# A Mamba-style mixer on one core: VectorE's work inside a phase put in another order

## Chip, cores and metric

One NeuronCore of a Trainium2 chip runs the whole program in one launch. The metric is the device time of one execution in microseconds (us), as a median of runs. PE is the matrix engine TensorE, DVE is VectorE, ACT is ScalarE, POOL is GpSimd and SP is the engine that issues most DMAs.

## What is computed

Four residual blocks follow one another on x (1024 tokens by 512, as 2 sequences b of 512), all in float32. The third takes most of the time:

```python
x = x + block_sparse(layernorm(x))     # weight masked in 32x32 blocks, plus bias
x = x + ffn(layernorm(x))              # dequantised int weights, 512 -> 1792 -> 512
x = x + mixer(layernorm(x))            # 128 heads of 64 channels, state of 128, 8 groups
x = x + ffn(layernorm(x))
# mixer, of one head, with chunks of 128 tokens:
xc, B, C = silu(conv4(x_proj)), silu(conv4(B_proj)), silu(conv4(C_proj))
y = (mask * exp(decay) * (C B^T)) @ (dt*xc)  +  C @ states * exp(decay)  +  D*xc
out += (rmsnorm(y) * norm_w * silu(gate)) @ out_w
```

## The kernel before

**Tiles and phases.** The 8192 channels of the mixer are 64 tiles of 128. A *phase* `ph` handles two of them for both sequences, so four *units* (j, b): tile j, sequence b. `units` (line 782) lists them as (0,0), (0,1), (1,0), (1,1). Phases are pipelined three deep. In one pass of the loop at line 1156 PE does four things: the input projection of the new pair of tiles (`x_front`), the scan of the pair before it, the output projection of the pair before that (`out_seven`, 14 small products called `o()`), and the gate projection of the new pair (`g_front`).

**Seven products.** A projection for two tiles and two sequences is a Strassen-Winograd scheme, `seven` (line 177): a generator of seven products (x, y, z, then y, x, y, z again, adding to the same three PSUM banks). Between them ACT copies the first one (L202) and DVE adds (L206 after the second product; L211 and L212 after the fourth; L220 after the sixth; L225 after the seventh). The fourth and sixth products write into a bank that DVE has just read, so the fourth waits for L206 and the sixth for L211.

**A unit's work.** `conv` (ACT, L731) and three taps on DVE (L734, queued in a list and issued by `drain(n)`), then `silu` (ACT). `x_tokens` (called `tokens(k)`, k an index into `units`) turns the x tile into tokens with four PE transposes (L827) into a PSUM bank with the tag "tr", of which there are two; DVE multiplies it by dt (L831), POOL by the decay (L835). `states` makes the chunk states on PE (L848) and carries them from chunk to chunk on DVE (one copy L859 and four small operations L862). `scores` makes the decays of one head on ACT (L892, L899, L902); their product with the masked C B^T, L900, is put into the list `mults` and issued by `flush()`, which empties the list; POOL multiplies `ce` (L906). `scan` is 28 small matmuls of a unit (L919, L928); `skipped` adds D*xc (L939) and `gated` multiplies by the gate (L942), both on DVE. `squares` adds y squared (ACT L948, POOL L949); its y buffer is one of three.

**Kinds of phase.** Every fourth phase also projects B and C of the next group (`group`, another seven products on PE with 12 taps); here it is called a *group phase* (`new_group`, ph = 3, 7, ... 27). The phase after it makes that group's masked C B^T in `group_scores` (a *post-group phase*). The other 15 phases from 2 to 30 are called *plain*. The branch `if mid:` (line 1216) holds the order of all of these.

**What sets the order.** `manual_schedule` (line 1540) keeps PE, ACT and DVE in the order in which the program issues, so a waiting instruction holds up all that follows on its engine. POOL and SP are ordered by the framework.

**Ends.** In `block_sparse` the weight's four row blocks are masked by `masked(kc)` (line 322): a row sum on DVE, a small matmul `pb`, a comparison and a multiplication L333, for the last block on POOL. After the last phase the code from line 1459 finishes the mixer: the last pair's output projections (`last_outs(t)`, 8 of them), the residual and norm of token tiles 0 to 3 (`rest`, `ahead`) and their transposes (`turn`).

Of the kernel before, what the change touches and what calls it, by code (L numbers as in the profile page):

```python
# [11 lines left out]
ALU = mybir.AluOpType  # L12
AX = mybir.AxisListType

P = 128
# [18 lines left out]
PP = 2  # L34
# [3 lines left out]
def kernel(  # L38
# [251 lines left out]
    def block_sparse():  # L290

        with tc.tile_pool(name="bs", bufs=1) as pool:
# [29 lines left out]
            def masked(kc):  # L322
# [9 lines left out]
                eng = nc.gpsimd if kc == KC - 1 else nc.vector  # L332
                eng.tensor_tensor(wv, wv, on.unsqueeze(2).to_broadcast([P, NB, 32]), ALU.mult)  # L333
# [18 lines left out]
            normed = [h() for h in halves]  # L352
            next(mask[0])
            for n in normed:
                turn(n)
            next(mask[0])
            pos = [bs_o() for _ in range(2)]
            for kc in range(KC):
                product(0, pos[0], kc)
                if kc + 1 < KC:  # L360
                    next(mask[kc + 1])
                product(1, pos[1], kc)
                if kc + 1 < KC:
                    next(mask[kc + 1])
# [304 lines left out]
    def mixer(waiting, step_args, loaded):  # L669

        with ExitStack() as st:
# [110 lines left out]
            units = [(j, b) for j in range(PP) for b in range(2)]  # L782
# [60 lines left out]
            def states(ct, b, x_dec, b_tok, by_act):  # L843
# [12 lines left out]
                if by_act:  # L856
                    nc.scalar.copy(state[:, 0], pst[:, 0])
                else:
                    nc.vector.tensor_copy(state[:, 0], pst[:, 0])  # L859
                for c in range(1, NCH - 1):  # L860
                    for hh in range(2):
                        nc.vector.scalar_tensor_tensor(  # L862
                            state[:, c, hh, :],
                            state[:, c - 1, hh, :],
                            e_last[:, b, c - 1, h0 + hh : h0 + hh + 1],
                            pst[:, c, hh, :],
                            ALU.mult,
                            ALU.add,
                        )
                return state  # L870
# [7 lines left out]
            def flush():  # L878
                for f in mults:
                    f()  # L880
                mults.clear()
# [274 lines left out]
            for ph in range(1, n_ph + 1):  # L1156
# [23 lines left out]

                def tokens(k):
# [3 lines left out]
                def both_states(k, by_act=False):  # L1185
                    for j, b in units[2 * k : 2 * k + 2]:
                        sts[j, b] = states(c1 + j, b, xts[j, b][1], groups[c1 // CTG][b][1], by_act)
# [26 lines left out]
                tokens(0)  # L1214
                tokens(1)
                if mid:
# [8 lines left out]
                    tokens(2)  # L1225
                    tokens(3)
                    flush()
                    o()
                    next(steps)
                    back_scores(2)  # L1230
                    o()
# [397 lines left out]
```

## Time and profile before

| | |
|---|---|
| median of 3 runs | 2297.31 us (2296.64 to 2298.96) |
| the profiled execution's own time | 2297.72 us |
| its span, first to last instruction | 2296.0 us |
| PE / DVE / POOL / ACT busy | 98% / 81% / 56% / 51% |
| span of a post-group phase, two plain ones and a group phase, one after the other | 52.10, 48.70, 49.20, 61.60 us |
| DVE busy in those four | 46.12, 45.08, 45.75, 54.86 us |

Times inside the profile are counted from the start of its span. A fenced line of a timeline gives start, duration, engine, line of the kernel, operation and tiles, the number of instructions put together, and in brackets how long the engine sat idle before them and on whom it waited. A line of the waits gives who waited for whom: the sum in us, how often, the longest. A row of the windows gives a stretch and its length, then each engine's busy time with its number of instructions, TensorE's granted clock, the DMA engines' busy share and GB/s. Matmuls overlap in the records, so the spacing of their starts tells more than their duration.

### The profile page before, as it was taken

The numbers are of one execution on the slowest core, as the hardware profiler recorded it, in microseconds if no ns is written. First come the engines' busy times: TensorE is split into PE (matmuls) and PEld (weight loads), VectorE is DVE, ScalarE is ACT, GpSimd is POOL, SyncE is SP. The second block draws the span as 40 slices with busy tenths as digits, with TensorE's granted clock in tenths as the row PEclk, the third lists the DMA queues.
The fourth block names the chain that finished last, engine by engine and source line by source line (L and its number), as shares of the span: only waits on it lengthen the run. The fifth ranks groups of instructions, "written<-read, shape, count | busy, mean of one in ns | idle before, by whom it ended". The sixth has DMA issues, their size and how long they took to land.

```text
span 2296.0 us, 30153 instructions
## 1 busy us (share of the span) xinstructions
PE 2248.0 (98%) x10704; PEld 1403.4 (61%) x10704; DVE 1850.8 (81%) x3103; ACT 1168.9 (51%) x2474; POOL 1277.3 (56%) x1203
## 2 busy tenths in 40 slices
PE   9999999999999999999999999999999999999999
PEld 5444865656665665666666656665666666544468
DVE  5456568888998999899889989998998899865553
ACT  4111056756565665666566656655665666631100
POOL 3665024756655666566657565665675665527620
PEclk9999999999999999999999999999999999999999
DMA  5663022222222222222222222221222322427600
GB/s 178 196 199 113 24 70 64 74 73 66 74 74 65 74 78 79 65 74 83 65 74 69 70 73 70 77 85 56 83 74 65 101 74 74 120 83 226 203 21 28
DMA packets 145783, 201.59 MB, mean 88 GB/s; under 512 B 7136, under 2 KB 92000, under 8 KB 145632
## 3 DMA queue, kind: packets, MB, share of 16 engines
q1 hardware_dynamic: 145056, 198.61, 27.0%
q8 instruction: 85, 1.39, 0.2%
q10 hardware_dynamic: 576, 1.05, 0.1%
q14 instruction: 66, 0.54, 0.1%
HBM read 194.91 MB, written 4.72 MB: 87 GB/s over the span
## 4 chain that ended last, share of the span: by engine, by line
PE 77%; DVE 20%; ACT 2%; issue 1%; DMA 1%; POOL 0%; ACTq 0%; SPq 0%; POOLq 0%; DVEq 0%
PE proj L185 25%; PE po L1020 13%; PE yo L185 13%; PE ffn_o L556 7%; DVE m L900 5%; PE py L919 4%; PE pst L848 3%; DVE xc L734 3%; PE py L928 3%; DVE x_sb L1034 2%; DVE gt L942 2%; PE x_tr L827 2%; PE po L956 2%; PE pg L486 1%; PE pu L486 1%
## 5 line engine op out<-in xcount | busy, mean ns | idle before, releaser
L906 POOL TENSOR_TENSOR ce<-ce,c_t 128x384 f32<-128x384 f32 x256 | 299.5, 1174 | 343.0 <-ACT ce L902 337.2
L185 PE MATMUL proj<-xn_t,w 128*128 128x512 f32 x824 | 384.6, 593 | 2.0 <-DVE gt L206 1.7
L892 ACT ACTIVATE m<-bc,acs 128x128 f32<-128x128 f32 x1024 | 324.8, 389 | 8.3 <-PE py L919 8.2
L900 DVE TENSOR_TENSOR m<-m,gm 128x512 f32<-128x512 f32 x256 | 254.0, 1010 | 16.4 <-ACT m L899 16.4
L185 PEld LDWEIGHTS proj<-xn_t,w 128*128 128x128 f32 x824 | 153.0, 190 | 146.4 <-issue 136.0
L1034 DVE TENSOR_TENSOR x_sb<-x_sb,po 128x512 f32<-128x512 f32 x340 | 229.7, 682 | 15.6 <-PE po L1020 9.6
L734 DVE SCALAR_TENSOR_TENSOR xc<-proj,cw,xc 128x511 f32<-128x511 f32 (+2 forms) x288 | 214.8, 746 | 6.6
L171 POOL TENSOR_TENSOR ws<-w 128x256 f32<-128x256 f32 x96 | 72.9, 759 | 238.3 <-DMA w<-in_win_t_dram 195.5
L185 PE MATMUL proj<-tq,ws 128*128 128x512 f32 x432 | 199.3, 592 | 0.0
L919 PE MATMUL py<-m,x_dt 128*64 128x128 f32 x2048 | 189.1, 277 | 3.3 <-DVE m L900 3.2
L949 POOL TENSOR_TENSOR sq_acc<-sq_acc,y 128x512 f32<-128x512 f32 x128 | 179.6, 1406 | 20.9 <-ACT y L948 20.8
L1020 PE MATMUL po<-wo,gt 128*128 128x256 f32 x696 | 177.0, 384 | 0.0
L899 ACT ACTIVATE m<-m 128x512 f32<-128x512 f32 x256 | 161.3, 630 | 7.4
L185 PE MATMUL yo<-xn_t,w 128*128 128x512 f32 x328 | 152.5, 597 | 9.0 <-DVE tmp L206 7.3
L185 PE MATMUL yo<-tq,ws 128*128 128x512 f32 x336 | 154.0, 601 | 0.2 <-ACT acs L714 0.2
L928 PE MATMUL py<-ce,state 128*64 128x128 f32 x1536 | 154.1, 273 | 0.0
L919 PEld LDWEIGHTS py<-m,x_dt 128*64 128x64 f32 x2048 | 130.8, 137 | 36.8 <-issue 25.8
L948 ACT ACTIVATE y<-y 128x512 f32<-128x512 f32 x128 | 76.5, 622 | 140.5 <-DVE gt L942 140.5
L1020 PEld LDWEIGHTS po<-wo,gt 128*128 128x128 f32 x696 | 125.4, 190 | 30.8 <-issue 9.4
L245 POOL TENSOR_TENSOR w<-w,sf 128x1024 f32<-128x1024 f32 (+1 forms) x30 | 70.0, 2335 | 111.8 <-DVE w L244 86.1
L902 ACT ACTIVATE ce<-bc 128x384 f32<-128x384 f32 x256 | 129.7, 507 | 0.0
L185 PEld LDWEIGHTS proj<-tq,ws 128*128 128x128 f32 x432 | 81.8, 190 | 76.7 <-issue 73.7
(227 smaller groups left out, 4585.1 us busy)
## 6 DMA issues: line engine op xcount, KB each, us to landing
bc<-acs_d SPq DMA_DIRECT2D x128, 512.0 KB, 3.8
w<-in_win_t_dram SPq DMA_DIRECT2D x64, 512.0 KB, 3.8
wo<-in_wo_t_dram SPq DMA_DIRECT2D x31, 512.0 KB, 5.0
wi<-in_down_w_dram SPq DMA_DIRECT2D x14, 512.0 KB, 3.8
zi<-in_down_z_dram SPq DMA_DIRECT2D x14, 512.0 KB, 4.7
sf<-in_down_s_dram SPq DMA_DIRECT2D x14, 512.0 KB, 4.3
wi<-in_gate_w_dram SPq DMA_DIRECT2D x13, 512.0 KB, 4.2
zi<-in_gate_z_dram SPq DMA_DIRECT2D x13, 512.0 KB, 5.2
```

Source lines behind the costliest of these rows:

```text
L185: nc.tensor.matmul(ps, lhsT=a[:, kc, :], rhs=b[:, kc, :], start=(start and kc == 0), stop=(stop and kc == KH - 1), skip_group_check=True,)
L556: nc.tensor.matmul(ps, lhsT=a[:, k, :], rhs=b(k), start=(start and k == 0), stop=(stop and k == KF - 1), skip_group_check=True,)
L734: nc.vector.scalar_tensor_tensor(dst[:, s:], ps[:, : SEQ - s], cw[:, t, 3 - s : 4 - s], dst[:, s:], ALU.mult, ALU.add)
L892: nc.scalar.activation(m[:, c, :], bc[:, hh, c * P : (c + 1) * P], AF.Relu, bias=acs[:, t, h : h + 1], scale=-1.0,)
L899: nc.scalar.activation(m, m, AF.Exp, scale=-1.0)
L900: mults.append(lambda: nc.vector.tensor_mul(m, m, shared[b][2]))
L906: nc.gpsimd.tensor_mul(ce, ce, c_t[:, P:].rearrange("p (c l) -> p c l", l=P))
L919: nc.tensor.matmul(py[hh * HD : (hh + 1) * HD, c * P : (c + 1) * P], lhsT=x_dt[:, c, hh, :], rhs=m[:, c, :], start=True, stop=(c == 0),)
L928: nc.tensor.matmul(py[hh * HD : (hh + 1) * HD, c * P : (c + 1) * P], lhsT=state[:, c - 1, hh, :], rhs=ce[:, c - 1, :], start=False, stop=True,
L949: nc.gpsimd.tensor_add(sq_acc[:, b, :], sq_acc[:, b, :], y)
L1020: nc.tensor.matmul(banks[k][:, c, :], lhsT=a[:, t], rhs=b, start=(start and c == 0), stop=stop, skip_group_check=True,)
L1034: nc.vector.tensor_add(q, q, banks[k])
```

## The change

In a phase between the second and the next to last: the list of units becomes (0,0), (1,1), (1,0), (0,1). The x tiles are turned after the first input product and the first output product, the second two after the second of each, and no longer around the first. The states of the second two units are made on PE where they were, or after `group_scores` in a post-group phase, but carried on DVE later, between the output products that follow the first scan. `flush(n)` can issue a part of `mults`. Both `gated` of the first scan come later, with one `squares` each. The first *two* products of the gate projection come ahead of the second scan; in a group phase the group's seven products come there with `gated` and `mults` between them. Both `gated` of the second scan come after both `skipped`. One of two `mults` of the next pair is left to the next phase. `group_scores` of the second sequence moves to the end of a post-group phase. In `block_sparse` all four multiplications are DVE's and each row sum is issued earlier; after the last phase the norms, transposes and squares stand in another order.

```diff
@@ -329,8 +329,7 @@
...
                 wv = wt[:, kc].rearrange("p (b j) -> p b j", j=32)
-                eng = nc.gpsimd if kc == KC - 1 else nc.vector
-                eng.tensor_tensor(wv, wv, on.unsqueeze(2).to_broadcast([P, NB, 32]), ALU.mult)
+                nc.vector.tensor_tensor(wv, wv, on.unsqueeze(2).to_broadcast([P, NB, 32]), ALU.mult)
                 yield
...
@@ -350,18 +349,20 @@
...
             normed = [h() for h in halves]
             next(mask[0])
+            next(mask[1])
             for n in normed:
...
             for kc in range(KC):
+                if kc + 2 < KC:
+                    next(mask[kc + 2])
                 product(0, pos[0], kc)
...
                 product(1, pos[1], kc)
-                if kc + 1 < KC:
-                    next(mask[kc + 1])
             ahead = norm(2, True)()
...
@@ -779,7 +780,8 @@
...
 
-            units = [(j, b) for j in range(PP) for b in range(2)]
+            units = [(0, 0), (1, 1), (1, 0), (0, 1)]
 
...
@@ -840,7 +842,7 @@
...
 
-            def states(ct, b, x_dec, b_tok, by_act):
+            def states(ct, b, x_dec, b_tok):
 
...
@@ -853,21 +855,21 @@
...
                 state = wrk.tile([P, NCH - 1, 2, HD], F32, name="state", bufs=4)
-                if by_act:
-                    nc.scalar.copy(state[:, 0], pst[:, 0])
-                else:
+                def carried():
                     nc.vector.tensor_copy(state[:, 0], pst[:, 0])
-                for c in range(1, NCH - 1):
-                    for hh in range(2):
-                        nc.vector.scalar_tensor_tensor(
-                            state[:, c, hh, :],
-                            state[:, c - 1, hh, :],
-                            e_last[:, b, c - 1, h0 + hh : h0 + hh + 1],
-                            pst[:, c, hh, :],
-                            ALU.mult,
-                            ALU.add,
-                        )
-                return state
+                    for c in range(1, NCH - 1):
+                        for hh in range(2):
+                            nc.vector.scalar_tensor_tensor(
+                                state[:, c, hh, :],
+                                state[:, c - 1, hh, :],
+                                e_last[:, b, c - 1, h0 + hh : h0 + hh + 1],
+                                pst[:, c, hh, :],
+                                ALU.mult,
+                                ALU.add,
+                            )
+                return state, carried
 
...
@@ -875,10 +877,12 @@
...
 
-            def flush():
-                for f in mults:
+            def flush(n=None):
+                n = len(mults) if n is None else min(n, len(mults))
+                for f in mults[:n]:
                     f()
-                mults.clear()
+                del mults[:n]
 
...
@@ -1178,13 +1182,22 @@
...
 
+                def a_square():
+                    squares(*ys.pop(0))
                 def tokens(k):
...
 
-                def both_states(k, by_act=False):
+                def both_states(k, now=True):
+                    carry = []
                     for j, b in units[2 * k : 2 * k + 2]:
-                        sts[j, b] = states(c1 + j, b, xts[j, b][1], groups[c1 // CTG][b][1], by_act)
+                        sts[j, b], carried = states(c1 + j, b, xts[j, b][1], groups[c1 // CTG][b][1])
+                        if now:
+                            carried()
+                        else:
+                            carry.append(carried)
+                    return carry
 
...
@@ -1211,8 +1224,6 @@
...
                     wbc = load_group((c0 + PP) // CTG)
-                tokens(0)
-                tokens(1)
                 if mid:
...
@@ -1222,19 +1233,21 @@
...
                     next(steps)
-                    tokens(2)
-                    tokens(3)
-                    flush()
                     o()
+                    tokens(0)
+                    tokens(1)
                     next(steps)
...
                     o()
+                    tokens(2)
+                    tokens(3)
                     o()
...
                     next(steps)
-                    flush()
+                    flush(len(mults) - 1)
                     both_states(0)
                     o()
+                    flush()
                     next(steps)
...
@@ -1245,64 +1258,96 @@
...
                     run(steps)
-                    both_states(1)
+                    if not made:
+                        carry = both_states(1, False)
                     scans = half_scan(units[:2])
...
                     o()
-                    flush()
                     back_scores(5)
                     o()
+                    flush(1)
                     o()
-                    o()
-                    gated[0]()
-                    flush()
                     back_scores(6)
...
                     o()
-                    flush()
+                    flush(1)
+                    if made:
+                        carry = both_states(1, False)
+                    carry[0]()
+                    o()
                     back_scores(7)
-                    if made:
-                        group_scores(made, groups[c0 // CTG], [1])
                     o()
-                    flush()
-                    gated[1]()
-                    all_squares()
-                    made = None
+                    carry[1]()
+                    gate, later = g_front(wg, gts_new, "proj" if new_group else ("proj", "yo", "yo"))
                     if new_group:
...
                         steps, made = group((c0 + PP) // CTG, wbc, "yo")
-                        for i, _ in enumerate(steps):
-                            if i in (1, 3, 5):
-                                drain(3)
-                        gate, later = g_front(wg, gts_new)
+                        next(steps)
+                        flush(1)
+                        gated[0]()
+                        flush(1)
+                        next(steps)
+                        drain(3)
+                        a_square()
+                        next(steps)
+                        next(steps)
+                        drain(3)
+                        gated[1]()
+                        a_square()
+                        next(steps)
+                        next(steps)
+                        run(steps)
+                        drain(3)
                     else:
-                        gate, later = g_front(wg, gts_new, ("proj", "yo", "yo"))
+                        next(gate)
+                        flush(1)
+                        gated[0]()
+                        flush(1)
+                        half_scores(0, c0, heads_new)
+                        a_square()
                         next(gate)
...
                     wo = load_out(ph - 1)
-                    finish(half_scan(units[2:], "tr"))
+                    scans = half_scan(units[2:], "tr")
+                    scans[0][0]()
+                    if new_group:
+                        scans[1][0]()
+                        next(gate)
+                        half_scores(0, c0, heads_new)
+                        next(gate)
+                    else:
+                        gated[1]()
+                        scans[1][0]()
+                    half_scores(1, c0, heads_new)
+                    if not new_group:
+                        a_square()
+                    for _, f in scans:
+                        f()
                     if ph < n_ph - 2:
                         lefts, rights = out_left(gts), out_right(wo)
-                    if new_group:
-                        next(gate)
-                    half_scores(0, c0, heads_new)
-                    next(gate)
                     drain(3)
-                    half_scores(1, c0, heads_new)
+                    for u in units[:2]:
+                        silu(xcs_new[u], xcs_new[u])
                     next(gate)
                     next(gate)
+                    flush(1)
+                    if made and not new_group:
+                        group_scores(made, groups[c0 // CTG], [1])
+                        made = None
+                    silu(xcs_new[units[2]], xcs_new[units[2]])
                     drain(3)
-                    for u in units:
-                        silu(xcs_new[u], xcs_new[u])
-                    flush()
+                    silu(xcs_new[units[3]], xcs_new[units[3]])
+                    next(gate)
                     next(gate)
...
                 else:
+                    tokens(0)
+                    tokens(1)
                     next(steps)
...
@@ -1489,35 +1534,27 @@
...
             back_scores(7)
+            flush()
             factors(0)
+            first_rest = rest(0)
             last_outs(2)
-            flush()
-            half = rest(0)
-            def ahead(t):
-                nonlocal half
-                new = rest(t + 1)
-                normed = half()
-                half = new
-                return normed
             scans = half_scan(units[2:], "proj")
-            normed = ahead(0)
+            second_rest = rest(1)
+            normed = first_rest()
             finish(scans)
...
             turn(normed)
-            normed = ahead(1)
+            normed = second_rest()
+            all_squares()
             last_outs(4)
+            halves = [rest(2), rest(3)]
+            last_outs(5)
             turn(normed)
-            normed = ahead(2)
-            last_outs(5)
-            all_squares()
-            turn(normed)
-            normed = half()
+            normed = [h() for h in halves]
             last_outs(6)
-            turn(normed)
+            turn(normed[0])
             last_outs(7)
+            turn(normed[1])
             for f in adds:
...
             factors(1)
```

## The prediction

> **What bounds the kernel now.** I read first the page's busy times, then the waits of PE, then the windows of four successive phases, then one plain phase's timeline of DVE and PE.
>
> ```profile
> PE 2248.0 (98%) x10704; PEld 1403.4 (61%) x10704; DVE 1850.8 (81%) x3103; ACT 1168.9 (51%) x2474; POOL 1277.3 (56%) x1203
> ...
> L900 DVE TENSOR_TENSOR m<-m,gm 128x512 f32<-128x512 f32 x256 | 254.0, 1010 | 16.4 <-ACT m L899 16.4
> ```
>
> PE is idle for 2296.0 - 2248.0 = 48.0 us in all. No reordering can give much more than that: the floor is near 2248.
>
> ```profile
> PE x_tr L827 <- DVE x_dt L831: 14.6, 21, 1.2
> PE yo L185 <- DVE tmp L206: 7.3, 7, 1.0
> PE ln_tr L142 <- ACT tmp L127: 4.2, 3, 2.2
> PE py L919 <- DVE m L900: 3.2, 15, 0.2
> PE bs_o L337 <- POOL wt L333: 1.9, 1, 1.9
> PE yo L185 <- DVE gt L206: 1.8, 8, 0.3
> ```
>
> Most of PE's waits are for DVE: for the second pair of x tiles (both "tr" banks full until L831), and for L206. These are what the change aims at.
>
> ```profile
> 828.30:877.50 49.20, 48.54 (x266) 31.55 (x265) 45.75 (x77) 31.26 (x69) 32.90 (x32) 1.00 0.24 75
> ```
>
> In this plain phase DVE is busy for 45.75 of 49.20 us. It has only 3.4 us to spare, so what it does while PE scans matters as much as PE's own gaps.
>
> ```profile
> 850.77 0.29 DVE L859 COPY state<-pst 128x128 f32<-128x128 f32 x1
> ...
> 853.98 0.75 DVE L939 SCALAR_TENSOR_TENSOR y<-xc,dsk,py 128x512 f32<-128x512 f32 x1 [0.28 <-PE py L928]
> ...
> 859.65 1.50 DVE L900 TENSOR_TENSOR m<-m,gm 128x512 f32<-128x512 f32 x1
> ...
> 867.34 1.68 DVE L942 SCALAR_TENSOR_TENSOR gt<-y,nw,gt 128x512 f32<-128x512 f32 x1
> ...
> 871.76 0.68 DVE L211 TENSOR_TENSOR gt<-gt,yo 128x512 f32<-128x512 f32 x1
> ```
>
> The carries (L859, L862) now fill DVE while PE does the first scan (850.55 to 853.76); from its second y (853.98) to the gate projection's L211 (872.44) DVE hardly rests. That chain of 18.46 us is the thing to follow.
>
> **The change, part by part.** The sum is made against the profiled execution's 2297.72 us, 1.7 of it outside the span; the median is 0.4 less.
>
> *Plain phases (15).* Matmuls are neither added nor removed. Today's waits of PE, from the spacing of its starts in this phase: 0.53 at the turn of x; 0.65 in the second scan (3.86 us against 3.21 for the first); 0.37 before the gate's fourth product. The phase before it has the last two only, so 1.3 on the mean. The turn's wait goes: x_dt then has an input product, an output product and eight transposes of cover (1.72 + 0.86 + 0.87 us). If that cover failed, the 0.53 would come back. The gate's wait for L206 goes too, as 3.2 us of scan now lie behind its second product.
>
> What is late next is L211. In the new order DVE does between its second y and L211 all that it does now (seven adds, four m, four gt, two y, one L206, three taps), and also both carries, which leave the shadow of the first scan. A carry takes 1.09 us (850.77 to 851.86), two 2.18. The y itself can't come earlier, since it waits for the scan: DVE idles there instead, in a gap that was the carries'. The four m and four gt last 8.46 us in this phase; with the page's mean of 1.010 and the groups' mean of 0.959 for L942 they last 7.88, so 0.58 less. Chain: 18.46 + 2.18 - 0.58 = 20.06 us. It starts 3.43 us after the first scan starts, so L211 ends at 23.5. PE would reach the gate's sixth product, which needs L211, at 873.20 - 850.55 - 0.65 - 0.37 = 21.6. It waits 23.5 + 0.1 - 21.6 = 2.0, against 1.3 now: +0.65 a phase, +9.8 in all. Part of that wait may fall earlier, where the second scan's last unit needs the fourth m (about 15.3 against 14.7); it is the same chain and counts once.
>
> [...] the change moves `gated` towards its own squares on POOL. The rows: m 0.68 alone (863.35), 1.50 beside POOL, 1.010 on the mean. [...] I take the row's mean.
>
> The other moves: the two flushes of the next pair's m become one before and one after the phase's end (0.7 to 1.0 us; at the start DVE idles 1.1 us at its L206, which hides it; uncovered it costs its full time, once a phase). The y buffers (three): the fourth y needs the first one's square; that ends, with ACT's 2.3 us of scores ahead and POOL's 1.4, near 17, and is needed near 17.8: nothing, up to 0.5 if ACT is late. `half_scores` takes its DMA of bc along (3.8 us to landing on SP, which the program doesn't order): no ACT wait for it is in the trace, so nothing. `load_pair` and `load_out` stand behind two products instead of one; POOL's sums for the output (four of 1.27 us) start some 2 us later and end about when the next phase starts, 5 us before their use: nothing, or the excess.
>
> *Post-group phases (7).* PE waits 1.38 + 0.16 at the turn and 0.40 in `group_scores`: 1.9. The second `group_scores` lies in the stretch before the sixth product, 1.3 us of cover more, and `group_scores` before the states adds as much, so L211 is not late. But the group phase ends with six taps ahead of L220, so DVE is free 1.9 us later than now; ACT's gate and group silus (eight of 0.6 us), squares and copy follow, and x's L206 slips from 7.0 to 8.6 us into the phase. DVE idles there and x's own L211 comes 0.7 to 0.8 late. So -1.9 + 0.75 = -1.15 a phase, -8.1 in all. From both sides: -1.9 to 0.
>
> *Group phases (7).* The turn's 0.5 goes. Group L206: DVE has gt less and two carries more, and no longer waits 1.17 for ACT's copy behind the squares: it ends near 15.9 after the scan's start, when PE wants it at 14.8. The 1.2 wait stays. Late taps ahead of the gate's L211 cost some 0.4. Sum about 0; from -1.7 to +1.
>
> *The start.* The last block's mask moves from POOL, behind two bias additions, to DVE (0.7 us).
>
> ```profile
> 15.10 1.10 PE L337 MATMUL bs_o<-wt,xn_t 128*128 128x512 f32 x2
> 18.12 3.57 PE L337 MATMUL bs_o<-wt,xn_t 128*128 128x512 f32 x4 [1.91 <-POOL wt L333]
> ...
> 16.00:24.00 8.00, 4.70 (x12) 2.10 (x12) 4.20 (x15) 3.07 (x7) 3.64 (x4) 0.79 1.09 349
> ```
>
> The four matmuls behind the wait take 3.36 us from start to start, 1.72 elsewhere, and the granted clock is 0.79. [...] The row shows the drop after 1.9 us, so both go: 2.1 + 1.6, and 0.3 of smaller gaps: -4.0. The second row sum now stands ahead of the first transposes (+0.6, in that sum). If later tiles of x aren't there yet (DMA is fully busy up to 24), only -1 is left.
>
> *The end.* Waits for ACT's normalised tiles: 0.76, 2.38; for gt 0.48; and some seven slow matmuls (granted clock 0.89 from 2018 to 2033), 1.7: 5.3 in all. In the new order each norm has an output projection more (1.72 us) ahead of its transposes; the wait for gt grows to 0.9. So -4.5; between -2 and -5.5.
>
> Sum: +9.8 - 8.1 + 0 - 4.0 - 4.5 = -6.8: 2290.9 in the profile's terms, 2290 as a median. Its own range is 2280 to 2300.
>
> **The rivals.**
> *The chain is hidden.* If m and gt meet POOL seldom (eight at 0.69 to 0.75 = 5.8), the chain is 18.46 - 8.46 + 5.8 + 2.18 = 18.0, L211 ends at 21.4, before PE wants it. Then plain phases lose all 1.3 (-19.5), post-group 1.9 (-13.3), group about 1.1 (-8); with the ends -49: 2248. For it: POOL has a free stretch where `gated` now stands. Against it: POOL is busy 32.9 of 49.2 us, and squares follow `gated`.
> *The carries make it slower.* Place: DVE between second y and L211; price: 1 us a plain phase for each us of chain over 18.2, and it turns slower once the chain passes about 20.5. With m and gt as long as in this phase: 20.64, wait 2.6, +1.3 x 15 = +19; the same lateness takes half of the post-group gain (-4) and +1 in each group phase (+7); with the ends -8.5: +14, 2311. For it: both m and gt are met by POOL in this phase; DVE idles beside the scan. Against it: one phase is not the mean.
> *It does nothing.* The waits change names, and the ends are bound by DMA at the start and by the residuals at the end: 2297.
>
> **Chances.** Forecast 0.40, hidden 0.20, slower 0.28, nothing 0.12. A measurement of this kernel can tell about 0.2% (4.6 us) from no change. Of the forecast 0.32 lies below 2292.7, with 0.19 of the hidden: faster 0.51; same 0.07 + 0.11 + 0.02 = 0.20; slower 0.29. The range, 2260 to 2312, leaves out half of the hidden case and a third of the slower.
>
> **What would show it.** Right: no row of PE L827 waiting on L831; DVE idle before L939 at the first scan; PE waiting on gt L211 before the sixth gate product, about 2 us in plain phases; bs_o without its POOL wait and with clock 1.00; plain phases near 49.6, post-group near 51. Wrong: plain phases at 47.6 (hidden) or at 50.2 and more (slower), a new wait on bc, on y's squares or on POOL's sums.

## The result, and the profile after

The changed kernel takes 2392.99 us (median of 4 runs, 2385.59 to 2396.38), against 2297.79 (2296.64 to 2298.96) for the kernel before in the same comparison. The ratio is 1.041, 95% interval 1.0385 to 1.0435: slower by 95 us, where 2290 was forecast.

The page of the changed kernel gives the busy times, and its group row of the m products:

```profile
PE 2277.0 (95%) x10704; PEld 1413.4 (59%) x10704; DVE 1846.4 (77%) x3104; ACT 1167.0 (49%) x2474; POOL 1277.1 (53%) x1202
...
L904 DVE TENSOR_TENSOR m<-m,gm 128x512 f32<-128x512 f32 x256 | 245.6, 971 | 0.0
```

The span is 2394.7, so PE is idle for 117.7 us, 69.7 more than before. But PE is also *busy* for 29.0 more with the same 10704 matmuls. The two make up the whole 98.7 us of difference in span. DVE does the same amount of work. The m and gt products together last 374.7 us, against 376.8 before, so products that last longer beside POOL are not the cause.

The waits of PE (waiting engine and tile, engine and line waited for: sum, times, longest):

```profile
PE yo L185 <- DVE gt L211: 70.8, 22, 4.5
PE po L1024 <- DVE x_sb L1038: 10.3, 18, 0.8
PE proj L185 <- DVE gt L211: 4.1, 7, 0.6
PE pst L850 <- ACT b_tok L773: 4.0, 7, 0.6
```

The row of x_tr waiting on x_dt is gone, as the change wants. In its place stands one row that is larger than all of the waits of before together: the gate's sixth product waits for L211, 3.2 us on the mean in each of 22 phases. What makes L211 late is read from DVE's own waits:

```profile
DVE y L943 <- PE py L932: 39.5, 49, 1.2
DVE y L943 <- PE yo L185: 34.9, 10, 3.5
...
DVE y L943 <- POOL sq_acc L953: 23.7, 11, 3.5
```

The first line is the gap beside the first scan that the forecast expected. The other two are one wait, 58.6 us in 21 places, all before a y of the second scan. A wait is named after the last of several semaphores. In about half of these places that is PE, whose fourth gate product happens to end within 0.05 us of POOL's sum of squares; but y reads nothing of that product. In all 21 places y starts 0.033 to 0.035 us after POOL's sum, while its distance from the end of PE's product lies anywhere up to 0.43. So POOL's is the true name, and e1 tests it below. One plain phase shows it (DVE's timeline; the first scan starts at 873.93):

```profile
877.35 0.75 DVE L943 SCALAR_TENSOR_TENSOR y<-xc,dsk,py 128x512 f32<-128x512 f32 x1 [0.78 <-PE py L932]
...
887.85 0.75 DVE L946 SCALAR_TENSOR_TENSOR gt<-y,nw,gt 128x512 f32<-128x512 f32 x1
888.51 0.68 DVE L904 TENSOR_TENSOR m<-m,gm 128x512 f32<-128x512 f32 x1
889.12 0.68 DVE L206 TENSOR_TENSOR gt<-gt,yo 128x512 f32<-128x512 f32 x1
889.72 0.74 DVE L943 SCALAR_TENSOR_TENSOR y<-xc,dsk,py 128x512 f32<-128x512 f32 x1
890.37 0.78 DVE L946 SCALAR_TENSOR_TENSOR gt<-y,nw,gt 128x512 f32<-128x512 f32 x1
894.64 0.75 DVE L943 SCALAR_TENSOR_TENSOR y<-xc,dsk,py 128x512 f32<-128x512 f32 x1 [3.49 <-PE yo L185]
895.31 2.48 DVE L946 SCALAR_TENSOR_TENSOR gt<-y,nw,gt 128x512 f32<-128x512 f32 x2
897.71 2.31 DVE L735 SCALAR_TENSOR_TENSOR xc<-proj,cw,xc 128x511 f32<-128x511 f32 x3
899.93 0.68 DVE L211 TENSOR_TENSOR gt<-gt,yo 128x512 f32<-128x512 f32 x1
```

The fourth y (894.64) could have started at 891.15. It needs the buffer of the first y, which comes free when that one has been multiplied (887.85), squared by ACT (888.63 to 889.26) and added up by POOL. POOL's timeline in the same stretch (wo is the tile of output weights that `load_out` fetches):

```profile
887.94 1.86 POOL L992 TENSOR_TENSOR ws<-wo 128x256 f32<-128x256 f32 x1 [4.53 <-DMA wo<-in_wo_t_dram]
889.88 0.73 POOL L993 TENSOR_TENSOR ws<-wo,ws 128x256 f32<-128x256 f32 x1
890.57 1.18 POOL L994 TENSOR_TENSOR wo<-wo 128x256 f32<-128x256 f32 x1
891.70 0.72 POOL L995 TENSOR_TENSOR ws<-wo,ws 128x256 f32<-128x256 f32 x1
892.38 0.99 POOL L910 TENSOR_TENSOR ce<-ce,c_t 128x384 f32<-128x384 f32 x1
893.34 1.27 POOL L953 TENSOR_TENSOR sq_acc<-sq_acc,y 128x512 f32<-128x512 f32 x1
```

The square was ready for POOL at 889.26 and is taken at 893.34. The framework, which orders POOL, had put it behind the four small sums of the output weights' quarters (`out_right`; called the sides from here on), and before the first of these POOL stood idle for 4.53 us until wo had landed. At 894.61 the buffer is free, at 894.64 the y starts.

PE then pays twice. Its timeline at the sixth product, and the windows of the wait and of the eight matmuls behind it (PE, PEld, DVE, ACT, POOL busy; then the granted clock):

```profile
900.66 2.97 PE L185 MATMUL yo<-tq,w 128*128 128x512 f32 x4 [4.32 <-DVE gt L211]
```

```profile
896.30:900.60 4.30, 0.04 (x1) 0.00 (x0) 4.23 (x5) 0.56 (x1) 3.59 (x4) 1.00 0.00 0
900.60:905.90 5.30, 5.24 (x9) 2.22 (x10) 4.36 (x7) 1.46 (x4) 2.69 (x2) 0.68 0.18 39
```

After the idle 4.3 us the granted clock is 0.68: several matmuls start 0.85 us apart instead of 0.43. Such matmuls follow 18 of the 22 waits, some 1.7 us each time, and they are the extra busy time.

The same plain phase as a row of the windows (the forecast's fence has one of before, 49.20 us long), and the start of the program:

```profile
853.93:908.48 54.55, 49.85 (x266) 32.30 (x265) 43.91 (x76) 31.21 (x70) 32.67 (x32) 0.97 0.22 68
```

```profile
16.00:24.00 8.00, 6.61 (x23) 3.19 (x22) 5.86 (x19) 4.84 (x11) 4.78 (x4) 1.00 1.09 347
```

The plain phase is 5.4 us longer with DVE busy for less of it. At the start PE does 6.61 us of work where it did 4.70, at clock 1.00 instead of 0.79: that part came as forecast.

### The profile page after: what moved, and what is told of

Its sections match the earlier page's. It is cut to its first block, busy times and chain, and to the rows that moved or that the text cites. A ratio compares the mean times of both kernels' runs of the same rounds, so it can differ in the third digit from the quotient of the medians.

```text
span 2394.7 us, 30173 instructions
## 1 busy us (share of the span) xinstructions
PE 2277.0 (95%) x10704; PEld 1413.4 (59%) x10704; DVE 1846.4 (77%) x3104; ACT 1167.0 (49%) x2474; POOL 1277.1 (53%) x1202
## 4 chain that ended last, share of the span: by engine, by line
PE 72%; DVE 18%; ACT 3%; POOL 3%; DMA 3%; issue 1%; SPq 0%; POOLq 0%; DVEq 0%; ACTq 0%
PE proj L185 21%; PE yo L185 15%; PE po L1024 11%; PE ffn_o L557 7%; PE py L923 4%; PE pst L850 3%; DVE gt L946 3%; DVE xc L735 3%; PE py L932 3%; DVE x_sb L1038 2%; DVE m L904 2%; DMA wo<-in_wo_t_dram 2%; PE x_tr L829 2%; PE po L960 1%; DVE b_t L735 1%
## 5 line engine op out<-in xcount | busy, mean ns | idle before, releaser
L910 POOL TENSOR_TENSOR ce<-ce,c_t 128x384 f32<-128x384 f32 x256 | 280.5, 1100 | 366.2 <-ACT ce L906 360.3
L904 DVE TENSOR_TENSOR m<-m,gm 128x512 f32<-128x512 f32 x256 | 245.6, 971 | 0.0
L953 POOL TENSOR_TENSOR sq_acc<-sq_acc,y 128x512 f32<-128x512 f32 x128 | 173.9, 1369 | 40.2 <-ACT y L952 39.7
L943 DVE SCALAR_TENSOR_TENSOR y<-xc,dsk,py 128x512 f32<-128x512 f32 x128 | 94.1, 744 | 99.8 <-PE py L932 39.5
L185 PE MATMUL yo<-tq,w 128*128 128x512 f32 x168 | 102.6, 743 | 70.8 <-DVE gt L211 70.8
L750 ACT ACTIVATE xc<-xc 128x512 f32<-128x512 f32 x128 | 74.9, 623 | 188.2 <-DVE xc L735 187.9
```

Of the source, the lines that this page charges most:

```text
L185: nc.tensor.matmul(ps, lhsT=a[:, kc, :], rhs=b[:, kc, :], start=(start and kc == 0), stop=(stop and kc == KH - 1), skip_group_check=True,)
L904: mults.append(lambda: nc.vector.tensor_mul(m, m, shared[b][2]))
L910: nc.gpsimd.tensor_mul(ce, ce, c_t[:, P:].rearrange("p (c l) -> p c l", l=P))
L953: nc.gpsimd.tensor_add(sq_acc[:, b, :], sq_acc[:, b, :], y)
```

## The experiments

Theory A: the fourth y waits for a buffer whose release stands in POOL's queue behind operations that wait for wo. Theory B, the forecast's own rival: the carries and gate products that now come later make DVE late by themselves. A median of each kernel is given, and its ratio to the kernel before with the interval.

**e1, a y buffer for everyone.** The changed kernel; y is written over the x tile, which nothing reads after it.

```diff
-                y = y_room()
+                y = xc
```

> The changed kernel with one edit: the scan writes y into its own x tile (dead by then) and no longer into one of three shared y buffers. Theory A (y buffers): the fourth y of a plain phase waits 3.5 us on VectorE for the first y's buffer, which is free only when GpSimd has added its square, behind four operations that wait for the output weight's DMA. Without the shared buffers that wait is gone, TensorE's wait before the gate's sixth product falls from 4.5 us to 2 us or less, the slow matmuls behind it go, a plain phase takes 49 to 50.5 us and not 54.6: total 2280 to 2310. Theory B (the prediction's chain: the carries behind the scan make L211 late whatever the buffers do): VectorE would only meet the next thing, L211 stays 3 us late or more, total 2360 or more.

2307.27 us, 1.0041 (1.0028 to 1.0055): 86 of the 95 us are gone. Its waits of PE, and one of its longer plain phases:

```profile
PE yo L185 <- DVE gt L211: 12.9, 15, 1.5
PE po L1024 <- DVE x_sb L1038: 8.2, 13, 0.8
```

```profile
830.03:881.79 51.76, 48.85 (x265) 31.69 (x264) 46.37 (x76) 30.89 (x68) 34.14 (x34) 1.00 0.22 72
```

L211's row falls from 70.8 to 12.9, no y waits for POOL, PE is busy for 2245.0 us and the clock is 1.00. The span is 89.1 us shorter, of which 57.1 was idle time and 32.0 slow matmuls. The buffer is the cause; the carries and gate products are as late here as in the changed kernel.

**e12, the transfer alone.** The changed kernel with its three buffers. The tile of wo is loaded once and kept, so the four sides don't wait. The kernel leaves out the later phases' weights, so its output is not the reference's.

```diff
+            wo_kept = []
...
+                    if ph > 1:
+                        return wo_kept[0]
                     wo = sc.tile([P, PP, DIM], F32, tag="wo", name="wo")
+                    wo_kept[:] = [wo]
```

> The changed kernel with the output projection's weights read once (from the third phase's on, the tile is kept and its lower right side is only negated and added to again, so the output is not the reference's): GpSimd's four sides no longer wait for a transfer, and 512 KB less are moved in each phase. Theory A (the fourth y waits for a buffer whose release stands in GpSimd's queue behind four operations that wait for that transfer): the sum of squares comes 3.5 to 4.6 us earlier, VectorE's waits for it fall from 23.7 us in all to under 5, TensorE's wait for gt L211 from 70.8 to under 25, and the time to 2305 to 2335. Rival B (the late carries and gatings make VectorE late whatever GpSimd does): no more than 15 us of gain, 2375 to 2393. Rival C (the buffer is late because the gate product itself is late, and the sides of 3.3 us alone hold it up): 2340 to 2370.

2318.19 us, 1.0097 (1.0081 to 1.0112): 75 of the 95 us. The y of the second scan waits for POOL's sum once, 1.2 us. PE's wait, and POOL's timeline at the same place:

```profile
PE yo L185 <- DVE gt L211: 24.6, 22, 2.2
```

```profile
867.12 0.73 POOL L997 TENSOR_TENSOR ws<-wo 128x256 f32<-128x256 f32 x1 [0.77 <-PE po L1029]
867.92 0.73 POOL L998 TENSOR_TENSOR ws<-wo,ws 128x256 f32<-128x256 f32 x1
868.61 0.73 POOL L999 TENSOR_TENSOR wo<-wo 128x256 f32<-128x256 f32 x1
869.30 0.72 POOL L1000 TENSOR_TENSOR ws<-wo,ws 128x256 f32<-128x256 f32 x1
871.70 1.30 POOL L915 TENSOR_TENSOR ce<-ce,c_t 128x384 f32<-128x384 f32 x1 [1.68 <-ACT ce L911]
872.97 1.27 POOL L958 TENSOR_TENSOR sq_acc<-sq_acc,y 128x512 f32<-128x512 f32 x1
```

The order in the queue is the same, but POOL is through with the four sides before the square is due. So it is the transfer in front of them, not their 2.9 us, that holds the buffer. (The transfers of 512 KB a phase are missing too, which may have a part in it.)

**e3 and e11, gate products early.** The changed kernel with both `gated` of the first scan ahead of the gate's first product again (e3), or the first one alone (e11); the squares follow right behind that product.

```diff
                     flush(1)
                     o()
+                    gated[0]()
                     back_scores(6)
...
                         next(gate)
-                        flush(1)
-                        gated[0]()
-                        flush(1)
+                        flush(2)
+                        a_square()
                         half_scores(0, c0, heads_new)
-                        a_square()
                         next(gate)
```

(These are e11's lines; e3 moves `gated[1]()` too, behind `carry[1]()`.)

> The changed kernel with both gate products of the first scan, and their squares, back ahead of the gate's first product; carries stay late, the y buffers stay three. Theory A: the first square is added before the output weight's four operations on GpSimd, so the buffer is free in time: plain phases 49 to 51 us, total 2285 to 2320. Theory B: the carries are still in the chain, total 2360 or more.

> The changed kernel with only the first unit's gate product and square early; the second one, the carries and the three buffers stay as changed. Theory A: the fourth y needs just the first one's buffer, so this one move frees it: plain phases near 50.5, total 2300 to 2325, less than the 2339 of both gate products early, as the second isn't put ahead of the second scan. If all squares must be early, or the carries are the cause: 2340 or more.

2338.77 us, 1.0175 (1.016 to 1.0191), and 2333.80, 1.0156 (1.0143 to 1.017): both lie above the range expected. The buffer's wait is gone from DVE and the mean clock is 0.999 or more again, but another wait has grown, here in e11:

```profile
PE po L1024 <- DVE x_sb L1038: 26.5, 22, 1.5
PE yo L185 <- DVE gt L211: 15.0, 16, 1.2
```

The first gate product now stands ahead of the last three output adds, and PE waits for these (10.3 us in the changed kernel). Theory A had left out what the gate product costs at its old place in the new order: some 27 us against e1, of which this row explains 18.

**e4 and e8, carries early.** The carries of the second states directly behind them again, in the changed kernel (e4) and in e1 (e8).

```diff
                     if not made:
-                        carry = both_states(1, False)
+                        both_states(1)
...
                     if made:
-                        carry = both_states(1, False)
-                    carry[0]()
+                        both_states(1)
                     o()
                     back_scores(7)
                     o()
-                    carry[1]()
```

> The changed kernel with the carries of the second two states back beside the first scan; gate products stay late, y buffers three. Theory A: the buffer's release hangs on GpSimd and the DMA of the output weight, not on VectorE's load, so VectorE waits longer at the fourth y and little is won: total 2375 to 2395. Theory B: 2.2 us less in each of 22 chains and the clock kept: total 2300 to 2340.

> The changed kernel with y in its own x tile and the carries back beside the first scan. With the buffer wait gone (2307 with late carries) what is left is the predicted chain: 2.2 us less in it should take TensorE's waits for L211 (12.9 us) away and some of those of the output products (8.2): 2280 to 2295. If the carries' place is worth nothing once the buffers are free: 2305 to 2310.

2377.89 us, 1.0355 (1.0341 to 1.0369; L211's wait still at 65.5), as theory A expected, and 2312.41, 1.0064 (1.005 to 1.0078), above both expectations. Theory B falls: carries early win 15 of the 95 us with shared buffers and nothing with free ones, where they even seem to *cost* 5, though the interval touches e1's. The forecast had priced the late carries at +2.2 us of chain. In e8 PE's wait for the output adds is 16.3 us, against 8.2 in e1, and that for L211 18.5 against 12.9.

**e7, the late gate products in the kernel before.** Both `gated` and their squares behind the gate's first product and around the second scan's y, nothing else of the change.

```diff
-                    gated[0]()
...
-                    gated[1]()
-                    all_squares()
...
-                    finish(half_scan(units[2:], "tr"))
+                    gated[0]()
+                    all_squares()
+                    scans = half_scan(units[2:], "tr")
+                    scans[0][0]()
+                    gated[1]()
+                    scans[1][0]()
+                    all_squares()
+                    for _, f in scans:
+                        f()
```

> The kernel before with one part of the change: both gate products of the first scan, and their squares, after the gate's first product and inside the second scan. The three y buffers stay, but here the framework puts the first square's addition ahead of the output weight's four operations on GpSimd. Theory A (the late gate product hurts because its square stands behind the output weight's DMA on GpSimd): at most 1 us a plain phase, 2296 to 2315. Theory A2 (late gate products with three buffers hurt wherever the square stands): 3 us and a slower clock in some 20 phases, 2350 or more.

2325.86 us, 1.0122 (1.0108 to 1.0135), between the two expectations. DVE waits 38.0 us in 15 places for POOL's sum of squares, so the late products alone bring the buffer's wait. It depends on POOL's order. In plain phases but the first the framework puts the first square ahead of the four sides, and no y waits: these phases (47.8 and 48.9 us) are no longer than before. In post-group phases the square stands behind the four sides (53.7 to 58.6 us instead of 52.1). In group phases it stands behind the four sums for the next input weights (62.9 us instead of 61.8); in the one at 723.86, where y waits 3.33 us, POOL had waited 6.85 us for their transfer.

**e5 and e9, the parts that don't touch the buffers.** The kernel before with the change's start and end (e5), and with its later turns of the x tiles besides (e9).

```diff
-                tokens(0)
-                tokens(1)
...
                     next(steps)
-                    tokens(2)
-                    tokens(3)
                     flush()
                     o()
+                    tokens(0)
+                    tokens(1)
                     next(steps)
                     back_scores(2)
                     o()
+                    tokens(2)
+                    tokens(3)
```

> The kernel before with only the two ends of the change: the four masks on VectorE with row sums issued earlier, and the new order of norms, transposes and squares after the last phase. Prediction's terms: start -4.0, end -4.5 us, so 2289. The traces of before and after already differ by -3.7 up to the first turn of x and by -3.2 from the last one, so 2291. If the ends were bound by DMA and residuals: 2297.

> The kernel before with the two ends of the change (2291 by themselves) and the later turns of the x tiles, in the old order of units, with nothing else. Theory: the turn's wait (18 us from start to start in the kernel before) goes and nothing is put in its place, so 2274 to 2282. Rival: VectorE is loaded so fully that the wait turns up again at L211 or in the second scan: 2288 to 2294.

2291.15 us, 0.9973 (0.9964 to 0.9983), and 2284.88, 0.994 (0.9928 to 0.9953). The ends are worth 6.4 us of the 8.5 that were forecast. The turns give another 6, less than I had expected, since a new wait takes a part: PE for y at the first output product, 8.9 us in 8 places.

**e14, e15, e13: other parts on top of e9.** The gate's second product ahead of the second scan (e14), the order of units (e15), and both gate products late as in e7 with y over xc as in e1 (e13).

```diff
                         gate, later = g_front(wg, gts_new, ("proj", "yo", "yo"))
                         next(gate)
+                        half_scores(0, c0, heads_new)
+                        next(gate)
                     wx = load_pair(NCT + c0 + PP, NCT + c0 + PP + 1)
...
                     if new_group:
                         next(gate)
-                    half_scores(0, c0, heads_new)
-                    next(gate)
+                        half_scores(0, c0, heads_new)
+                        next(gate)
```

```diff
-            units = [(j, b) for j in range(PP) for b in range(2)]
+            units = [(0, 0), (1, 1), (1, 0), (0, 1)]
```

> The same kernel (2284.9) with the gate projection's second product and its half of the scores ahead of the second scan in plain and post-group phases. The prediction held that this takes away the wait for L206 (about 0.37 us in each of 22 phases, 8 us): 2274 to 2280. Rival: L211's chain is what binds, so the wait only moves: 2283 to 2290; and if the scores moved ahead of the scan make ACT late, above 2290.

> The same kernel (2284.9) with the change's order of units only. It changes which x tiles and scans come first, not what any engine does: 2282 to 2288. If it is a part of the 16 us by which the changed kernel with free buffers stands above the predicted 2290.6, then 2290 to 2300.

> The kernel with before's order, the change's start and end and its later turns of the x tiles (2284.9), with both gate products and squares of the first two units late as in the change, and y written over xc so that no y buffer is shared. If late gate products are good for the phase once buffers are free, as the carries were (about 5 us): 2272 to 2282. If gate products in the stretch before the gate projection's sixth product delay L206 and L211, as they did with shared buffers: 2290 to 2305.

e14: 2294.75 us, 0.999 (0.9981 to 0.9998), 10 more than e9. Its plain phases grow from 48.6 to 49.2 us, and two rows appear that e9 does not have:

```profile
PE yo L185 <- DVE gt L211: 17.8, 15, 1.6
DVE gt L206 <- ACT gt L202: 25.7, 22, 1.2
```

L211 is late because DVE now comes to L206 early and waits there for ACT's copy of the first gate product. In one plain phase (863.71) this copy stands behind a square, DVE idles for 1.17 us, and PE then waits 1.38 us for L211. Neither the changed kernel nor e1 has this wait, as there other work of DVE lies before L206, so e14 does not price the second product in the change's own order. e15: 2288.12, 0.9963 (0.995 to 0.9976), perhaps 3 more; they lie in phase 31 (55.5 us against 50.7 in e9), not in the plain phases (48.6 in both). e13: 2280.89, 0.9929 (0.9913 to 0.9946), the fastest of all, faster than both kernels. With buffers free, late gate products cost nothing.

**e16, e17, e18: what is left.** e16 is e9 with y over xc alone. e17 is e13 with the second states' carries behind the third and the fourth of the seven adds after the first scan (its expectation counted fourth and fifth), e18 behind the sixth and the seventh, in post-group phases not at all.

```diff
-                    both_states(1)
+                    carry = both_states(1, now=False)
...
                     o()
+                    carry[0]()
                     o()
+                    carry[1]()
                     o()
                     flush()
                     back_scores(6)
```

> The kernel with before's order, the change's start and end and its later turns (2284.9), with y written over xc and nothing else. If freeing the buffer is all that writing over xc does, it is worth nothing here, where VectorE waits for no y buffer: 2283 to 2287. If it has a gain or a price of its own: outside that, and e13's 2280.9 would be explained by it.

> The kernel of e13 (late gate products, y over xc, 2280.9) with both carries of the second states late as well, one each behind the fourth and the fifth of the output adds that follow the first scan (before them they stood ahead of the scan). If late carries are worth 5 us, as with the change's own order and free buffers: 2274 to 2279. If, as the prediction held, they lengthen the chain to L211 by 2.2 us in each of 22 phases: 2290 to 2310. If they only fill idle time either way: 2279 to 2283.

> The kernel of e13 (2280.9) with the second states' carries behind the sixth and the seventh of the seven output adds that follow the first scan, in plain and group phases; in post-group phases they stay ahead of the scan. (In e17 they stood behind the third and the fourth, which its expectation counted wrongly, and TensorE waited 1.9 us in each of 22 phases for the adds behind them.) If the place among the adds is what cost e17 its time: the wait for adds falls under 10 us in all and the time to 2275 to 2290. If it is the late carries as such, which leave VectorE idle beside the first scan and keep it late to the gate projection: 2310 to 2350, with TensorE's wait moved to L206 or L211.

e16: 2283.55 us, 0.994 (0.9926 to 0.9955), the ratio of e9. So writing y over xc has no gain of its own where no buffer is waited for, and what e1 won was the buffer. The step from e9 to e13 lies within the intervals.

e17: 2351.47 us, 1.0237 (1.022 to 1.0254), 70 more than e13, which none of the three expectations held.

```profile
PE po L1022 <- DVE x_sb L1036: 41.9, 22, 1.9
PE yo L185 <- DVE gt L206: 18.5, 22, 1.5
```

```profile
DVE xc L941 <- PE py L930: 74.6, 67, 2.6
```

PE waits in 22 phases for the adds behind the carries. In e18 (2296.50 us, 0.9993, 0.9985 to 1.0002) that row is gone and 55 of the 70 us with it, 6 of them because post-group phases are left alone; the others go with the place among the adds. But 16 remain: DVE's idle time beside the first scan is 51.8 us against 24.4 in e13, and plain phases are 48.9 instead of 47.7. Both my expectations for e18 missed. In this order late carries do cost time, as the forecast said, 1.2 us a plain phase. Why they cost nothing in the changed kernel's order, I could not settle.

## Why the prediction was wrong, point by point

**The step that failed: the y buffers.** It said "the fourth y needs the first one's square; that ends ... near 17, and is needed near 17.8: nothing, up to 0.5 if ACT is late". The profile after: needed at 891.15, 17.2 us after the scan's start, so that was right. ACT wasn't late either (square done at 15.3). But POOL's sum ended at 894.61, 20.7 after it. "POOL's 1.4" was the duration of the operation; the working had no term for what POOL would be doing when the square arrived. Yet the forecast itself noted that the framework orders POOL, and that the load has sums behind it. The four sides behind that load, and the squares behind these, were one queue; I priced the load as if nothing but the output sums depended on it. The load itself is not later than before. POOL's timeline of the kernel before, in the plain phase whose first scan starts at 850.55:

```profile
860.55 1.73 POOL L949 TENSOR_TENSOR sq_acc<-sq_acc,y 128x512 f32<-128x512 f32 x1
864.50 0.79 POOL L988 TENSOR_TENSOR ws<-wo 128x256 f32<-128x256 f32 x1 [2.22 <-DMA wo<-in_wo_t_dram]
```

There the first side starts 13.95 us after the scan, in the changed kernel 14.01. But there the first square is through before it; moved later on DVE, the square came behind the sides. POOL's wait for wo, 53.7 us in 23 places before, became 105.1 us in 27, and now it held up a buffer. The forecast's signs of being wrong did name "a new wait ... on y's squares", but no rival and no chance was built on it. That m lasts longer beside POOL (1.50 us against 0.68 alone, in the kernel before), which was weighed there, plays no part: the m and gt products last 374.7 us in all, against 376.8.

**The slow matmuls.** No step held that a wait of PE would slow the matmuls behind it, although the forecast had read just that in the start's row (clock 0.79 after 1.9 us) and then put a wait of 2.0 us into every plain phase. They are about a third of the loss (29.0 of 98.7 us).

**The chain.** Its length was sized well: from the second y to the end of L211, 20.06 us forecast; in the phase shown, 900.61 - 877.35 = 23.26 less the wait of 3.49 is 19.77. What it costs was less sure. Plain phases: +0.65 forecast; with free buffers (e1) phases 5 to 29 of this kind average 49.8 us against 48.9 before, +0.9. The wait for L211 is there in all 15, but it is 0.86 us on the mean and not 2.0; PE loses some time earlier, at the output adds and in the second scan. That the carries are the cause is not shown: e8 has them early and is no faster. So that the sizes come near each other is partly luck.

**Post-group phases.** Forecast -1.15 each; in e1 they last 52.2 us against 52.1 before. The waits at the turn went, but in one such phase the first states wait 0.38 for x_dt, and the second ones, which now follow `group_scores`, wait for its parts, 0.34 for gm and 0.57 for ACT's b_tok: 1.29 in place of the 1.9. That is 9 of the 17 us by which e1 lies above the forecast.

**Group phases.** Forecast 0; 61.8 us in e1 and before.

**Phases at both ends.** Not costed by themselves: phases 2 and 31 are 2.0 and 1.3 us longer in e1. That is some 3 more of the 17, the plain phases are another 3, and the ends 2.

**The ends.** -4.0 and -4.5 forecast; the first x tile is turned 3.7 us earlier, and the stretch from the last phase on is 3.3 shorter. e5 has both, with 6.4 us.

**The rivals.** The chain was not hidden. The rival on the slower side named the carries and 2311; the kernel is slower for another reason, so what that rival had right in its sign was luck.

## What to carry to other kernels

When a step is moved later, ask which buffer it releases, and follow the release through every queue to the one that wants the buffer: a small sum on GpSimd behind four operations that wait for a transfer cost 75 us here. A wait of the matrix engine can bring slow matmuls after it, and its price must count them: some 1.7 us behind 18 of 22 waits here. Where a reordering loses, free the shared buffer first and try its parts again: its ends and turns alone were worth 13 us.

## What the runs showed of the hardware

The clock did not fall after every wait, and not always after equal ones. In the changed kernel two waits of the same sixth product, of 1.95 and of 1.97 us, were followed by this:

```profile
565.62 2.44 PE L185 MATMUL yo<-tq,w 128*128 128x512 f32 x4 [1.95 <-DVE gt L211]
...
1926.59 1.98 PE L185 MATMUL yo<-tq,w 128*128 128x512 f32 x4 [1.97 <-DVE gt L211]
```

In the 5.4 us behind the first the granted clock was 0.68, behind the second 1.00. There are 22 such waits in this trace. All eleven of 4.3 us and more were followed by slow matmuls, and so were both of 2.92 and five of the seven between 1.95 and 1.97; the one of 2.15 and the one of 1.47 were not. So a wait's length alone does not tell, and what else decides these runs don't show. The mean granted clock was 0.986 in the changed kernel and 1.000 in e1, and e1 has PE busy for 32.0 us less.
